# Shifted scores six ticks behind the maxima's scores in place of seven, and the maxima's rows sent from ScalarE's queue

## The chip, the cores and the metric

The kernel runs on one core of one Trainium2 chip. The metric is the device time of one execution in microseconds; the runs of the kernel before have a median of 1069.59 us (1068.0 to 1072.75, three runs). One further execution was profiled. All row times below are from that one.

The core has five engines that work side by side, each with its own queue of instructions in a fixed order: TensorE (PE, matrix products; PEld is its loading of weights), VectorE (DVE), ScalarE (ACT), GpSimd (POOL) and SyncE (SP, which here only issues DMA transfers). They wait for each other by semaphores.

## The reference

Two transformer layers over x of 2 sequences x 1024 tokens x 128 features, in float32:

- layer 0, first part: retention with 8 heads (scores times a decay), group norm, a silu gate, a projection, then a layer norm over the sum with x;
- layer 0, second part: causal attention with 16 heads of 8 features (with latent keys and values and rotary positions), followed by a mixture of four experts, of which each token takes the best one; layer norm;
- layer 1, first part: full attention with 16 heads of 8 features, two entries masked; layer norm;
- layer 1, second part: a product with a weight rounded to -1, 0, 1; layer norm.

The change lies in the two attentions:

```
scores = einsum('bhqd,bhkd->bhqk', q, k) * scale
weights = softmax(scores, axis=-1)
out = einsum('bhqk,bhkd->bhqd', weights, v)
```

## The kernel before

**Stages.** Retention goes over chunks of 128 tokens until about 240 us into the span. From there to the end one long chain of attention runs (`chain_tick`, L568 on): all steps of layer 0's causal attention for sequence 0, then sequence 1, then those of layer 1. A step is (layer a, sequence b, half of the tokens k, group g of four heads, h: which 256 queries). There are 64 steps: 32 in each layer. A step is cut into items: in layer 1 four for each step, in layer 0 one to four. There are 208 items (`s_items`, `t_items`), and the two lists give each step the same places.

**Why scores are computed twice.** Softmax needs the maximum of each query's scores. The kernel first makes scores with queries on the partitions (`score`, tiles named sc), and VectorE takes their maxima (`maxima`, L425 for blocks on the diagonal, L430 for the others). When all of a step's items are in, `shifts` (L437) makes `lowered`, the negated maxima. `turn` (L444) transposes them on TensorE, `enter` (L446 to L452) copies the transposed rows out of PSUM on ScalarE (m_rows) and sends them by DMA into a spare row of qT for each head. With that row in the product, the second set of scores comes out already shifted by the maximum, and with keys on the partitions: `shifted`, tiles sct. ScalarE takes their exponentials (`exps`, L485, tiles es), and `product` multiplies them with the values (tile acc).

**Order of a tick.** The order on all engines is the order in which the code issues. Tick t takes the scores of item t and the shifted scores of item t - AHEAD. It makes them in two halves, so that two heads of the one run beside two other heads of the other on TensorE: sc of heads 0, 1 with sct of heads 2, 3, then sct of heads 0, 1 with sc of heads 2, 3 (`together`). Each half is followed by its maxima on VectorE and its exponentials on ScalarE. Then comes `shifts`, if the step's last item was this one. At the end of the tick stands `product` for item t - AHEAD - 1. If a step's scores ended with tick t - 1, that product also holds its `turn`, into a free part of the same PSUM tile, and then its `enter`: after the matmuls of acc ScalarE first copies m_rows, then acc (to oT for a step's first pair, L518, else to part, L521, which GpSimd adds, L522). Last, `finish` of a step stands at t_last + AHEAD + 3: it transposes the sums (o_ps), and for all but the last block (layer 1, sequence 1, second half of the tokens) every second step does so, with four transposes and a copy on ScalarE (ot, L538). In the last block each step does, with two transposes and no such copy.

So a step whose last item is l enters at the end of tick l + 1. In a step of four items (first item f = l - 3), its rows are needed at the start of tick f + AHEAD.

**PSUM.** All these tiles, and those of the side work, come in turn from a ring of eight banks (`ring_of`). A tile waits until the eighth tile before it has been read.

**Side work.** Projections, the experts and the outputs are generators, stepped by `side_work` before each tick. Each has a first tick and a tick by which it is due; `ends` (which holds AHEAD) and `starts` give these in ticks. Their transfers (`spread` L280, expert weights L1219 and others) are issued on SP, whose queue is in the order of the code. Before the change the 64 DMAs of L452 stand in that queue too. The transfers issued by SP and ScalarE take eight semaphores in turn, over both queues, in the order of the code; an issue may have to wait for the transfer that used its semaphore before.

Of the kernel before, what the change touches and what calls it, by code (L numbers as in the profile page):

```python
# [20 lines left out]
BQ = QT * P  # L21
RH, RD, RV = 8, 64, 128
NG, GH, HD = 4, 4, 8
HW = 32
ONE, NEG0, NEG1 = 8, 9, 10
# [5 lines left out]
NH = NG * GH  # L31
VW = HD + 1
VN = (NH - 1) * VW + HW
AHEAD = 7


def _columns(*parts):
# [27 lines left out]
def block_kernel(  # L65
# [13 lines left out]
    nc = tc.nc  # L79
# [20 lines left out]
    for e in range(NE):  # L100
# [6 lines left out]
        out=ahead, in_=ahead, pattern=[[1, P]], compare_op=ALU.is_gt, fill=0.0,  # L107
# [68 lines left out]
    qT, kT = ([early.tile([P, NG, T], F32, name=f"{name}_0")] for name in ("qT", "kT"))  # L176
# [179 lines left out]
    def queries(i):  # L356

        a, b, k, g, h = steps[i]
        return k * (BT // BQ) + h
# [5 lines left out]
    for i, (a, b, k, g, h) in enumerate(steps):  # L365
# [4 lines left out]
        else:  # L370
# [5 lines left out]
            if sum(piece[2] for piece in rest_of) <= BT:  # L376
                at, pieces = 0, []
# [68 lines left out]
    def enter(i, tp):  # L446

        a, b, k, g, h = steps[i]
        rows_of = small.tile([GH * QT, P], F32, tag="m_rows", name="m_rows", bufs=2)
        nc.scalar.copy(rows_of, tp[: GH * QT])  # L450
        at = queries(i) * BQ
        nc.sync.dma_start(out=qT[b][ONE::HW, g, at : at + BQ], in_=rows_of)  # L452

    def diagonal_pair(n_item):
        i, pair = t_items[n_item]
# [42 lines left out]
    def product(n_item, entering):  # L498

        i, pair = t_items[n_item]  # L500
        a, b, k, g, h = steps[i]
        acc = slot("acc")
        if entering is not None:
            turn(entering, acc[:, BQ : BQ + P])
        for r, (lo, at_) in enumerate(pair_of(n_item)):
            for j in range(GH):
                at = (g * GH + j) * VW
                mm(
                    acc[hrows(j), lo:BQ], v_aug[b][:, 2 * pair + r, at : at + HW],
                    es[n_item][:, j, at_ : at_ + BQ - lo], start=r == 0, stop=r == 1,  # L510
                )
        if entering is not None:
            enter(entering, acc[:, BQ : BQ + P])
        if pair == 0 and (h == 0 or by_half(a, b, k)):
            sums[a, b, k, g] = pools["work"].tile([P, BT], F32, tag="oT", name="oT")
        sum_ = sums[a, b, k, g][:, h * BQ : (h + 1) * BQ]
        if pair == 0:
            nc.scalar.copy(sum_, acc[:, :BQ])  # L518
        else:
            part = pools["work"].tile([P, BQ], F32, tag="part", name="part", bufs=2)  # L520
            nc.scalar.copy(part, acc[:, :BQ])  # L521
            nc.gpsimd.tensor_tensor(sum_, sum_, part, ALU.add)  # L522
# [35 lines left out]
    def step_of(*step):  # L558
        return steps.index(step)

    def ends(a, b, k, h=NQ - 1):

        return t_last[step_of(a, b, k, NG - 1, h)] + AHEAD + 4

# [3 lines left out]
    def chain_tick(tick):  # L568
        si = tick if tick < n_items else None
        ti = tick - AHEAD if 0 <= tick - AHEAD < n_items else None  # L570

# [18 lines left out]
        if 0 <= si < n_items and s_last[s_items[si][0]] == si:  # L590
            entering = s_items[si][0]
        ai = tick - AHEAD - 1
        if 0 <= ai < n_items:
            product(ai, entering)
        elif entering is not None:
            tp = slot("m_ps")[:, :P]
            turn(entering, tp)
            enter(entering, tp)
        ai = tick - AHEAD - 3
        if 0 <= ai < n_items and t_last[t_items[ai][0]] == ai:  # L600
# [3 lines left out]
    with ExitStack() as rc:  # L604
# [29 lines left out]
        at, n = R_CONST["cs"]  # L634
# [802 lines left out]
    for b in range(B):  # L1437
# [13 lines left out]
        for k in range(NB):  # L1451
            light.append(
                Job(ends(0, b, NB - 1), starts(1, b, 0) + 1, attn_inputs(b, k), made[k : k + 1])
            )
    last_tick = n_items + AHEAD + 4
    for b in range(B):
# [164 lines left out]
```

## Time and profile before

| what | value |
|---|---|
| median of the runs | 1069.59 us (1068.0 to 1072.75) |
| profiled execution, its whole time | 1073.1 us |
| its span from first to last instruction | 1071.4 us |
| mean granted TensorE clock | 0.983 |
| SP's issue of m_rows (L452), 64 of them | 520 / 548 / 633 ns (least, median, most) |
| ACT copy of m_rows (L450), 59 of them out of acc | 237 / 254 / 256 ns |
| exps (L485), 832 | mean 587 ns |
| copy of acc to part (L521), 144 | mean 394 ns |
| maxima (L430), 640 | mean 682 ns |

How to read it: the page gives each engine's busy time, then the chain of work that ended last, traced back from the last instruction to what released each step. Groups are named by engine, line and "out<-in" with the program's tile names. A line in the timeline has the start from the span's beginning, the time it lasted, engine, line, operation, tiles, shapes and how many; in square brackets the idle time of the engine just before it and who ended it. Nearly all matmuls carry L86, which is a helper; the tile's name tells them apart. A float32 product appears as two matmuls. Lines with ACTq or SPq are issues in that engine's queue and are not counted as busy.

### The profile page before, as it was taken

The page shows a single profiled execution, that of the slowest core. Times are in us where ns is not written, and L with a number is a line of the kernel's source. Part 1 is how long each engine was busy: PE and PEld are TensorE (multiplying, and loading weights), DVE is VectorE, ACT ScalarE, POOL GpSimd, SP SyncE. Part 2 cuts the span into 40 slices and gives each one's busy share as a digit, 9 for nine tenths or more (in the row PEclk, how much of TensorE's full clock was granted, in tenths as well). Part 3 has the DMA queues.
Part 4 walks back from the last instruction along what each step waited for, and adds up shares of the span by engine and source line. Part 5 has one row for each costly group of instructions (what it writes and reads, how often), then busy time and mean ns, then how long its engine had stood idle before and what let it go on. Part 6 is the DMA issues. An engine that isn't in the chain of part 4 may idle for free.

```text
span 1071.4 us, 28823 instructions
## 1 busy us (share of the span) xinstructions
PE 1013.0 (95%) x11510; PEld 722.8 (67%) x11510; DVE 772.6 (72%) x1765; ACT 689.7 (64%) x1492; POOL 459.9 (43%) x626
## 2 busy tenths in 40 slices
PE   6999999997899999989999999999999999999995
PEld 5888888874565657756766667666766666666662
DVE  4666786667785877777676776777677888888861
ACT  3555544544576767667666776667677777777774
POOL 3466454533355665374544434454333222222222
PEclk9999999997899999999999999999999999999998
DMA  6522122110101032004211032003211000000000
GB/s 207 148 56 50 40 50 51 25 27 2 29 1 22 12 98 81 22 12 107 81 29 21 2 108 60 27 18 115 61 29 22 2 13 2 13 2 2 12 3 10
DMA packets 32214, 44.82 MB, mean 42 GB/s; under 512 B 4624, under 2 KB 18384, under 8 KB 31952
## 3 DMA queue, kind: packets, MB, share of 16 engines
q1 hardware_dynamic: 30816, 40.59, 14.3%
q0 software_dynamic: 1024, 2.10, 0.7%
q8 instruction: 91, 1.49, 0.6%
q14 instruction: 43, 0.35, 0.1%
q10 hardware_dynamic: 240, 0.29, 0.1%
HBM read 25.60 MB, written 4.39 MB: 28 GB/s over the span
## 4 chain that ended last, share of the span: by engine, by line
PE 71%; DVE 12%; POOL 6%; DMA 4%; ACT 3%; issue 2%; SPq 1%; POOLq 0%; DVEq 0%; ACTq 0%
PE sc L86 17%; PE acc L86 16%; PE sct L86 14%; DVE spare L425 3%; PE ph L86 3%; PE pmoe L86 2%; DVE parts L430 2%; PE pr L86 2%; PE pout L841 2%; PE py L86 2%; PE pv L86 1%; PE o_ps L211 1%; ACT es L485 1%; PE mpr L86 1%; PE acc L444 1%
## 5 line engine op out<-in xcount | busy, mean ns | idle before, releaser
L485 ACT ACTIVATE es<-sct 128x512 f32<-128x512 f32 (+1 forms) x832 | 418.8, 587 | 168.1 <-PE sct L86 150.0
L430 DVE TENSOR_REDUCE parts<-sc 128x1 f32<-128x512 f32 x640 | 397.3, 682 | 99.0 <-PE sct L86 86.4
L86 PE MATMUL sc<-kT,qT 32*128 32x512 f32 (+3 forms) x1792 | 421.6, 580 | 7.9 <-DVE parts L425 4.3
L86 PE MATMUL sct<-qT,kT 32*128 32x256 f32 (+1 forms) x3328 | 405.8, 385 | 3.8 <-DMA qT<-m_rows 3.7
L86 PEld LDWEIGHTS sct<-qT,kT 32*128 32x128 f32 x3328 | 288.2, 185 | 24.7 <-issue 6.3
L522 POOL TENSOR_TENSOR oT<-oT,part 128x256 f32<-128x256 f32 x144 | 104.6, 726 | 336.0 <-ACT part L521 334.9
L86 PE MATMUL acc<-es,v_aug 128*32 128x256 f32 (+1 forms) x3328 | 217.9, 378 | 12.2 <-DVE parts L430 6.1
L86 PEld LDWEIGHTS sc<-kT,qT 32*128 32x128 f32 x1792 | 153.9, 187 | 77.7 <-issue 20.8
L86 PEld LDWEIGHTS acc<-es,v_aug 128*32 128x32 f32 x3328 | 88.8, 109 | 106.2 <-DVE parts L430 40.4
L425 DVE CUSTOM_DVE_ANT_0 spare<-sc,causal 128x128 f32<-128x128 f32 (+3 forms) x256 | 125.7, 491 | 46.2 <-PE sct L86 13.0
L909 ACT ACTIVATE og<-pt,cols_sb 128x128 f32<-128x128 f32 x124 | 45.0, 467 | 43.3 <-PE pt L896 43.3
L493 POOL TENSOR_SCALAR_AFFINE_SELECT es<-es 128x512 f32<-128x512 f32 x64 | 40.3, 635 | 61.3 <-ACT es L485 59.5
L521 ACT COPY part<-acc 128x256 f32<-128x256 f32 x144 | 56.7, 394 | 10.8 <-PE acc L86 8.5
L140 POOL TENSOR_TENSOR rstd<-rstd,nhalf 128x4 f32<-128x4 f32 (+2 forms) x46 | 55.6, 1209 | 3.7
L778 POOL TENSOR_TENSOR qd<-qk,r_rest 128x512 f32<-128x512 f32 x16 | 20.3, 1271 | 48.5 <-DVE qk L775 45.6
L795 ACT COPY v<-pv 128x1024 f32<-128x1024 f32 x16 | 16.2, 1012 | 38.1 <-PE pv L86 38.1
L772 POOL TENSOR_TENSOR swap<-swap,r_cs 128x1024 f32<-128x1024 f32 x15 | 35.4, 2357 | 10.0 <-DMA swap<-plain 10.0
L86 PE MATMUL py<-r_wo,og 128*128 128x128 f32 x256 | 33.3, 286 | 2.2 <-DVE og L994 2.2
L86 PEld LDWEIGHTS py<-r_wo,og 128*128 128x128 f32 x256 | 31.5, 200 | 3.2 <-PE xn_ps L211 1.0
L841 PE MATMUL pout<-v,sm 128*128 128x128 f32 x256 | 31.5, 276 | 1.1 <-DVE sm L809 1.1
L86 PE MATMUL pg<-xT,r_wg 128*128 128x128 f32 x256 | 31.4, 276 | 1.1 <-ACT v L795 1.1
L86 PEld LDWEIGHTS ph<-xgT,e_w 128*128 128x128 f32 x224 | 27.1, 191 | 7.8 <-issue 4.9
(235 smaller groups left out, 1284.7 us busy)
## 6 DMA issues: line engine op xcount, KB each, us to landing
e_w<-in_m_w SPq DMA_DIRECT2D x56, 256.0 KB
swap<-plain SPq DMA_DIRECT2D x62, 128.0 KB
qT<-dense SPq DMA_DIRECT2D x32, 64.0 KB
kT<-dense SPq DMA_DIRECT2D x32, 64.0 KB
e_in<-by_expert SPq DMA_DIRECT2D x4, 448.0 KB
from_expert<-e_out SPq DMA_DIRECT2D x4, 448.0 KB
x<-in_x SPq DMA_DIRECT2D x4, 256.0 KB
mcs<-in_m_const SPq DMA_DIRECT2D x4, 256.0 KB
```

Source lines behind the costliest of these rows:

```text
L86: nc.tensor.matmul(o, lhsT, rhs, start=start, stop=stop)
L140: nc.gpsimd.tensor_tensor(r, r, nhalf[:, :n], ALU.pow)
L425: nc.vector.tensor_tensor_reduce(out=spare[:, :n], in0=sc[:, at : at + n], in1=causal[:, BT - n :], scale=1.0, scalar=-3.0e38, op0=ALU.add ...
L430: nc.vector.tensor_reduce(part, sc[:, at : at + n], AX.X, ALU.max)
L485: nc.scalar.activation(es[n_item][:, j, :n], sct[:, :n], AF.Exp, scale=scale)
L493: nc.gpsimd.affine_select(out=d, in_=d, pattern=[[0, GH], [1, P]], compare_op=ALU.is_ge, fill=0.0, base=0, channel_multiplier=-1,)
L521: nc.scalar.copy(part, acc[:, :BQ])
L522: nc.gpsimd.tensor_tensor(sum_, sum_, part, ALU.add)
L772: engine.tensor_tensor(swap[n], swap[n], table(n, 1), ALU.mult)
L778: nc.gpsimd.tensor_tensor(qd[n], rq[n], gq, ALU.mult)
L841: nc.tensor.matmul(pout[n][:, a, g, :], sm[:, a, g, :], v[n][:, 2 * g + a, :], start=opens(n) and g == 0, stop=True, skip_group_check=True,)
L909: nc.scalar.activation(to, of, AF.Identity, bias=bias_, scale=weight)
```

## The change

AHEAD goes from 7 to 6, so each tick's shifted scores, exponentials, products and finishes are those of an item one place later; `last_tick` and `ends`, which hold AHEAD, move by one tick. And the DMA that sends the rows of maxima is issued by ScalarE, right behind its own copy of m_rows and ahead of its copy of acc.

```diff
-AHEAD = 7
+AHEAD = 6
...
         rows_of = small.tile([GH * QT, P], F32, tag="m_rows", name="m_rows", bufs=2)
         nc.scalar.copy(rows_of, tp[: GH * QT])
         at = queries(i) * BQ
-        nc.sync.dma_start(out=qT[b][ONE::HW, g, at : at + BQ], in_=rows_of)
+        nc.scalar.dma_start(out=qT[b][ONE::HW, g, at : at + BQ], in_=rows_of)
```

In the built program, the tick in which a step of four items enters now holds the product of the second pair of the step before it (copied to part), where it held the first pair (copied to oT), and every second such tick also holds the finish of a step. Of the 64 issues on ScalarE, 36 carry a wait for an earlier transfer besides the wait for m_rows.

## The prediction

> **What bounds the kernel now.** I read the page first: who is busy, and what the chain that ended last is made of.
>
> ```profile
> PE 1013.0 (95%) x11510; PEld 722.8 (67%) x11510; DVE 772.6 (72%) x1765; ACT 689.7 (64%) x1492; POOL 459.9 (43%) x626
> PE 71%; DVE 12%; POOL 6%; DMA 4%; ACT 3%; issue 2%; SPq 1%; POOLq 0%; DVEq 0%; ACTq 0%
> ```
>
> TensorE (PE) carries 71% of the chain, ScalarE (ACT) 3%. The sums of busy time by stretch sharpen this for the second layer's attention: of the 180 us from 850 to 1030, PE is busy 179.21 and ACT 136.17. There a stall of PE is time lost, nearly one to one. The chain of waits over one tick in which a step's maxima enter:
>
> ```profile
> 946.18 0.22 PE acc L444
> 946.40 1.00 PE acc L86 x16
> 947.40 0.42 PE sc L86
> ```
>
> The timeline of the same tick, all engines:
>
> ```profile
> 947.47 0.25 ACT L450 COPY m_rows<-acc 8x128 f32<-8x128 f32 x1
> 947.63 0.36 ACT L518 COPY oT<-acc 128x256 f32<-128x256 f32 x1
> 947.75 0.53 SPq L452 DMA_DIRECT2D qT<-m_rows  x1
> ...
> 948.31 0.59 PE L86 MATMUL sc<-kT,qT 32*128 32x512 f32 x2
> ...
> 948.67 2.07 ACT L485 ACTIVATE es<-sct 128x512 f32<-128x512 f32 x4 [0.68 <-PE sct L86]
> ```
>
> A tick takes nine PSUM tiles from a ring of eight banks: sc 0,1, sct 2,3, then sct 0,1, sc 2,3, then acc. So the acc of one tick gives its bank to the eighth tile of the next tick, an sc of its second half. That half starts at 948.31 and the copy that frees the bank ends at 947.63+0.36 = 947.99. The slack is 0.32 us; ACT's own idle time before the next exps is 0.68.
>
> **What the change removes.** First, waits for the rows. The list of waits, and SP's part of the timeline before the longest of them:
>
> ```profile
> PE sct L86 <- DMA qT<-m_rows: 3.7, 3, 1.9
> ```
>
> ```profile
> 323.44 2.12 SPq L280 DMA_DIRECT2D qT<-dense  x3
> 325.66 0.56 SPq L452 DMA_DIRECT2D qT<-m_rows  x1
> ```
>
> That step's rows were copied by 320.5, but their issue stood behind spreads on SP until 325.66, so they landed about 3.5 us later and PE waited 1.85. On ACT's queue the issue no longer stands behind spreads or expert weights: -3.7 us. SP itself is freed of 64 waits for ACT; no row shows PE waiting for expert weights, so I give that nothing.
>
> Second, one tick. With six in place of seven, the first shifted scores join the scores of tick 6 and one tick at the end goes. The chain of waits there:
>
> ```profile
> 1044.42 1.09 PE sct L86 x16
> 1045.51 1.16 PE acc L86 x16
> ```
>
> That is 1.09+1.16 = 2.2 us of PE alone. The same matmuls move into the start, where PE sat idle 2.08 us before the transpose at 269.04 while VectorE did maxima, and so are hidden there. If that cover failed, they would run in pairs with score matmuls and still save about 0.9 (a paired tick 2.94, less its acc 1.01, against 1.09 for sct alone and some 1.7 for sc alone, my estimate from its 8 passes). So -2.2, between -3 and -0.9.
>
> **What it adds.** 64 DMA issues on ACT. SP's issues of m_rows last 548 ns in the median. The nearest rows for ACT's own queue are the two swap issues at the start:
>
> ```profile
> 9.47 1.01 ACT L751 COPY plain<-pr 128x1024 f32<-128x1024 f32 x1 [6.92 <-PE pr L86]
> 10.52 1.24 ACTq L758 DMA_DIRECT2D swap<-plain  x2
> 11.80 1.01 ACT L751 COPY plain<-pr 128x1024 f32<-128x1024 f32 x1 [1.31 <-PE pr L86]
> ```
>
> 0.59 and 0.60 us each; no ACT work runs during them, though that copy's wait is also put down to PE. The issue must wait until m_rows is written, which SP did 0.03 us after the copy's end. Behind the waiting issue stand the copy of acc, sometimes the copy of o_ps, and the next exps; who waits is PE. In the tick shown: m_rows ends at 947.72, the issue runs 947.75 to 948.30, the acc copy starts at 948.34 in place of 947.63, a delay of 0.71.
>
> A rule speaks for the change here. The Trainium skill ("DMA: Bandwidth & Descriptors", "Issuing engines are not separate DMA queues") says that spreading issues over engines saves only the sequencer's initiating time, usually small beside the transfer, and its "Anatomy of one DMA" gives a sequencer dispatch of about 50 ns, on GpSimd's path. With 50 ns the delay would be 0.09 (the copy's overlap lost) +0.03+0.05 = 0.17, inside the slack of 0.32: no stall. With the row it is 0.71. I take the row, because it is this form of instruction on ACT; 0.17 and 0.71 remain the two ends.
>
> Now the stall per step. With six ticks, the entering tick no longer carries pair 0 but pair 1, so the copy is the part of 0.41: 948.34+0.41 = 948.75, and PE starts 0.05 later (the shortest distance from an ACT end to a PE start that waited for it). 948.80-948.31 = 0.49. In every second entering tick the finish of the step two before now falls too: PE does four transposes (0.59) first, ACT adds the copy of o_ps (0.58), and that copy holds an sc bank. Counted from 947.33 as zero: m_rows 0.14, issue over at 0.97, part 1.01 to 1.38, o_ps copy to 1.96, the second half at 0.59+0.98 = 1.57. Stall 1.96+0.05-1.57 = 0.44. The mean is about 0.46.
>
> How many steps are exposed I took from the trace by following, behind each of the 64 m_rows copies, the ACT instruction whose end frees a bank. Second layer, 32 steps: 7 are covered, because expert or projection work of PE follows or no scores are left. 18 of the ordinary steps are exposed: 18 x 0.46 = 8.3. In the last block, finished half by half, 7 steps have two transposes (0.37) in front and no copy of o_ps: 1.42+0.05-1.35 = 0.12 each, 0.8. First layer: 14 of 32 exposed, 14 x 0.46 = 6.4; but VectorE stands in the chain there too, so I count two thirds, 4.3. Sum +13.4.
>
> **Small terms.** A tick less of lead for the rows: in the second layer the time from issue to first use is about 6 us, becomes about 3, and the landing takes 1.6 (the semaphore's last update). It stays hidden in ordinary ticks; where weights are moving, landings took 3.1 to 5 us, and a tick there 3.5 to 5: +0.5. ACT's issue also waits, in 36 of 64 places by the built order, for an earlier DMA on the same semaphore. All but a few were issued over 6 us before, and expert weights landed in about 2.5 to 3.5; the nearest was issued 4.1 before: +0.5.
>
> Sum: -3.7-2.2+13.4+1.0 = +8.5. From the profiled span, 1071.4+8.5 = 1079.9; with the 1.7 that lies around it (1073.1), 1081.6. That execution stands 3.5 above the median of the runs, so the median goes from 1069.59 to 1078.
>
> **Rivals.** Hidden issue: ACT's engine is not held for the length of the issue. Its place is the gap between m_rows and the acc copy; below about 0.3 us no bank is late. Then only the gains remain, -5.9+0.5: 1064. This ends on the faster side, and decides at that gap. For it: the skill's rule, and ACT's 3% of the chain. Against it: the ACT rows, and the slack of only 0.32. Chance 0.22, half of it faster by over 0.5%.
>
> Everything exposed: in the jobs' ticks too, with their order moved by a tick, ACT is late for PE: 64 x 0.46 = 29, and lanes or landings 1 to 2. 29+2-5.9: 1095, or half of that excess, 1087, where the jobs hide some. Chance 0.2.
>
> No effect (a stall that VectorE's lag takes up everywhere in the first layer and half of it in the second): 9.1/2+1-5.9 = -0.3, 1069. Chance 0.1; it speaks against it that PE is at 179.21 of 180.
>
> **How the numbers follow.** The forecast (stalls of 0.3 to 0.6 a step) has 0.48: 1073 to 1085. 0.5%, 5.3 us, is about what a measurement here can tell from no change. Faster (below 1064.2): 0.12. Same: the other half of the hidden issue 0.1, no effect 0.1, the low edge of the forecast 0.04, so 0.24. Slower: 0.64. The range, leaving out the fastest of the hidden cases and the slowest of the exposed: 1063 to 1089.
>
> **What would show it.** Right: in the timeline of an entering tick, 0.6 us or more between m_rows and part on ACT; in the list of waits PE behind ACT part or ot, some 13 us where there was next to none; PE behind qT<-m_rows near nothing; a drain shorter by a tick. Wrong: part follows m_rows within 0.3; or PE's new waits name the rows' DMA, which would make the lost tick of lead the cause.

## The result, and the profile after

The changed kernel takes 1083.7 us (median of five runs, 1082.33 to 1086.28) where the kernel before takes 1069.98 beside it: 1.0119 of the time, 95% interval 1.0091 to 1.0147. It is slower, by some 13.7 us or 1.2%; the forecast was 1078, in a range of 1063 to 1089. The profiled execution took 1083.66 us (span 1081.9), at the median of its runs; that of before stood 3 us above its own, so the two spans differ by 10.5 only.

The page of the changed kernel, the same two lines as before:

```profile
PE 1023.2 (95%) x11510; PEld 728.0 (67%) x11510; DVE 774.3 (72%) x1765; ACT 697.2 (64%) x1492; POOL 459.8 (42%) x626
PE 66%; DVE 15%; POOL 7%; DMA 4%; ACT 4%; issue 3%; SPq 1%; ACTq 0%; POOLq 0%; DVEq 0%
```

Nothing there tells what happened: PE is as busy as ever, and ACT's queue has 0% of the chain. The timeline of a tick in which a step's rows enter does (all engines; the tick's first sc started at 957.57):

```profile
957.70 0.26 ACT L450 COPY m_rows<-acc 8x128 f32<-8x128 f32 x1
957.99 0.54 ACTq L452 DMA_DIRECT2D qT<-m_rows  x1
...
958.56 0.37 ACT L521 COPY part<-acc 128x256 f32<-128x256 f32 x1 [0.61 <-ACT m_rows L450]
...
958.99 0.18 PEld L86 LDWEIGHTS sc<-kT,qT 32*128 32x128 f32 x1 [0.25 <-ACT part L521]
959.00 0.70 PE L86 MATMUL sct<-qT,kT 32*128 32x256 f32 x4
```

ACT stands idle for 0.61 us around its issue, the copy of acc starts 0.86 us after that of m_rows (0.16 before the change), and TensorE's load of weights for the next sc waits for that copy's end. The next tick starts at 961.06: 3.49 us after this one, where the tick shown of before took 2.93. The chain of waits over the same tick:

```profile
958.49 0.22 PE sct L86 x3
958.71 0.76 PE sc L86 x2
959.47 0.22 PE sct L86 x3
```

A piece of sc that takes about 0.2 in other ticks takes 0.76: the stall is recorded as a long matmul, not as a gap. The sums by stretch show how far this hides it. Columns: stretch, its length, then busy time and number of instructions of PE, PEld, DVE, ACT and POOL, the granted clock, and two of DMA. First the kernel before, then the changed one:

```profile
850.00:1030.00 180.00, 179.21 (x2308) 117.58 (x2308) 152.67 (x298) 136.17 (x301) 48.94 (x68) 1.00 0.02 7
```

```profile
850.00:1030.00 180.00, 179.08 (x2237) 116.45 (x2233) 147.06 (x285) 134.89 (x290) 49.75 (x68) 1.00 0.02 7
```

The busy time of PE is the same, but it holds 71 matmuls fewer. The Trainium skill ("Perfetto Trace Analysis", "Identifying the Most-Contended Engine") warns that matmul busy time is a bad measure of how near TensorE is to its peak, and points to the share of its weight loads (among others); here those fall by 1%, from 117.58 to 116.45, and the count of matmuls, lower by 3%, says it more clearly than either.

The list of waits, changed kernel (total us, times, longest):

```profile
ACT part L521 <- ACT m_rows L450: 23.1, 38, 0.6
...
ACT oT L518 <- ACT m_rows L450: 11.5, 19, 0.6
...
PEld sc L86 <- ACT part L521: 6.4, 28, 0.4
...
PE sct L86 <- DMA qT<-m_rows: 1.4, 3, 0.7
```

and the third of these in the kernel before:

```profile
PEld sc L86 <- ACT part L521: 2.8, 9, 0.8
```

The first two are new: 57 gaps of 0.6 on ACT. The waits for the rows fell from 3.7 to 1.4 us. The chain at the end of the changed kernel:

```profile
1052.36 1.61 DMA qT<-m_rows
...
1054.11 1.38 PE sct L86 x14
...
1056.49 1.09 PE sct L86 x16
1057.58 1.05 PE acc L86 x16
```

One such pair (1.09+1.05) has gone from the end, but the last step's rows now land on the chain: PE waited 0.34 us for them.

Set beside each other by the start of a tick's first matmul, the changed kernel is 4.9 us behind at tick 144 (of 208), 12.2 at tick 208, 10.5 at the end. So most of the loss, 7.3 us, comes with the last 64 ticks, which have the least side work.

### The profile page after: what moved, and what is told of

It is laid out like the page before. It is cut to its first block, busy times and chain, and to the rows that moved or that the text cites. A ratio compares the mean times of both kernels' runs of the same rounds, so it can differ in the third digit from the quotient of the medians.

```text
span 1081.9 us, 28716 instructions
## 1 busy us (share of the span) xinstructions
PE 1023.2 (95%) x11510; PEld 728.0 (67%) x11510; DVE 774.3 (72%) x1765; ACT 697.2 (64%) x1492; POOL 459.8 (42%) x626
## 4 chain that ended last, share of the span: by engine, by line
PE 66%; DVE 15%; POOL 7%; DMA 4%; ACT 4%; issue 3%; SPq 1%; ACTq 0%; POOLq 0%; DVEq 0%
PE sc L86 16%; PE acc L86 15%; PE sct L86 12%; DVE spare L425 4%; DVE parts L430 3%; PE ph L86 3%; PE pmoe L86 2%; PE pr L86 2%; PE pout L841 2%; ACT es L485 2%; PE pv L86 1%; PE py L86 1%; PE o_ps L211 1%; PE psc L86 1%; PE acc L444 1%
## 5 line engine op out<-in xcount | busy, mean ns | idle before, releaser
L86 PE MATMUL sc<-kT,qT 32*128 32x512 f32 (+3 forms) x1792 | 433.1, 575 | 10.6 <-DVE parts L425 5.1
L86 PE MATMUL sct<-qT,kT 32*128 32x256 f32 (+1 forms) x3328 | 413.0, 386 | 1.4 <-DMA qT<-m_rows 1.4
L86 PEld LDWEIGHTS sct<-qT,kT 32*128 32x128 f32 x3328 | 284.5, 185 | 20.2 <-ACT part L521 1.5
L86 PEld LDWEIGHTS sc<-kT,qT 32*128 32x128 f32 x1792 | 159.8, 185 | 90.7 <-DVE parts L430 18.7
L518 ACT COPY oT<-acc 128x256 f32<-128x256 f32 x64 | 24.9, 390 | 14.6 <-ACT m_rows L450 11.5
```

The costliest lines, as they stand in the source:

```text
L86: nc.tensor.matmul(o, lhsT, rhs, start=start, stop=stop)
```

## The experiments

Theory 1: the issue holds ScalarE ahead of its copy of acc, and TensorE waits for that bank. Theory 2: the lost tick costs, by less lead for the rows or by the finish that falls into the entering tick. Theory 3: the cost lies in the transfer (ScalarE's ring, the shared semaphores, the landing). All ratios are against the kernel before on the same chip; absolute times differ from chip to chip.

**The queue alone** (act7).

```diff
-AHEAD = 6
+AHEAD = 7
```

> The new queue alone: rows issued by ScalarE, still seven ticks. Theory 1 (the issue holds ScalarE for 0.54 us ahead of the copy of acc, and TensorE waits for the bank): TensorE's stall is the same as in the changed kernel, some 15 us gross, less the 3.7 us of waits for the rows that go: 1080 to 1083 us. Theory 2 (the lost tick costs, by less lead or by the finish falling into the entering tick): nearly nothing is left but the gain of 3.7 us: 1066 us.

1.0141 (1.0118 to 1.0165). No wait for rows is left, and TensorE waits for ScalarE's copies:

```profile
PEld sc L86 <- ACT oT L518: 9.0, 26, 2.1
```

An entering tick lasts 3.50 us where it lasted 2.94. The queue costs the whole of it without the lost tick; against theory 2. It came out a little above what I expected, and in the profile one tick (93) is 3.9 us longer than before: at 627.78 the rows were written, but their issue started only at 629.49, because it waited for the semaphore of an earlier transfer of expert weights. The copy of acc behind it was held for that too:

```profile
ACT oT L518 <- DMA e_w<-in_m_w: 2.3, 1, 2.3
```

That is a piece of theory 3. The changed kernel has no such wait: each of its 64 issues started 0.03 us after its rows were written.

**The lost tick alone** (sp6).

```diff
-AHEAD = 7
+AHEAD = 6
```

> Six ticks alone: rows still issued by SyncE. Theory 1: no ScalarE gap, a tick less at the end (-2 us), but the four steps whose rows were held up behind spreads and weights on SyncE now lack one more tick of 3.3 to 4 us each: TensorE behind the rows' DMA grows from 3.7 to about 17 us, 1076 to 1084 us. Theory 2: besides that every step pays for the order, above 1085 us, with the entering ticks of the last 180 us longer than 3.1 us.

1.0112 (1.0089 to 1.0134). The list of waits:

```profile
PE sct L86 <- DMA qT<-m_rows: 13.4, 4, 5.3
```

SP's part of the timeline in front of one of the four waits:

```profile
390.96 2.82 SPq L280 DMA_DIRECT2D kT<-dense  x4
393.89 0.56 SPq L452 DMA_DIRECT2D qT<-m_rows  x1
```

Rows that stand behind four spreads on SyncE miss a tick of lead. The three ticks with the long waits last 18.1 us longer together than in the same order of work with the rows on ScalarE's queue (act6_last below), which is more than the 15.1 us that lie between the two forms at tick 208. So this half of theory 2, less lead for the rows, holds while the rows are on SyncE. The entering ticks of the last part keep their length (2.94 at tick 149). So each half of the change alone is slower by more than 1%, for different reasons: six ticks need another queue for the rows, and that queue, at that place, costs as much.

**The issue behind the copy of acc** (act6_late, and with seven ticks act7_late).

```diff
-        nc.scalar.dma_start(out=qT[b][ONE::HW, g, at : at + BQ], in_=rows_of)
+        return lambda: nc.scalar.dma_start(
+            out=qT[b][ONE::HW, g, at : at + BQ], in_=rows_of
+        )
...
-            enter(entering, acc[:, BQ : BQ + P])
+            send = enter(entering, acc[:, BQ : BQ + P])
...
             nc.scalar.copy(part, acc[:, :BQ])
             nc.gpsimd.tensor_tensor(sum_, sum_, part, ALU.add)
+        if entering is not None:
+            send()
...
```

> The change, but with ScalarE's issue moved behind its copy of acc. The same instructions, so the same ScalarE time. Theory 1: the bank comes free 0.7 us earlier and the issue falls into ScalarE's idle time of 0.6 us before the next exps: the stall goes, 1064 to 1067 us. Theory 2, and also a theory in which ScalarE's total load counts: no change against the changed kernel, 1080 to 1084 us.

> As the last, with seven ticks. Theory 1: only the waits for the rows (3.7 us) are gone against the kernel before: 1066 us, about 2 us above the six-tick form. Theory 2: 1066 us too, but then the six-tick form with the late issue stands at 1080.

Six ticks 1.0000 (0.9983 to 1.0018), seven ticks 0.9974 (0.9959 to 0.9988). Moving one instruction of ScalarE past its neighbour takes the stall away, though ScalarE's load is the same. The timeline of an entering tick, six ticks:

```profile
952.43 0.26 ACT L450 COPY m_rows<-acc 8x128 f32<-8x128 f32 x1
952.60 0.36 ACT L523 COPY part<-acc 128x256 f32<-128x256 f32 x1
...
952.72 0.54 ACTq L452 DMA_DIRECT2D qT<-m_rows  x1
```

The issue begins 0.03 us after m_rows is written, while part is still being copied. But the six-tick form stayed behind the forecast of 1064 to 1067 us: it should have been 0.2% to 0.5% faster than before. In the last part every second entering tick was still long, 3.34 us at tick 153 against 2.98 in the six-tick form with rows on SyncE.

**The issue at the end of the tick** (act6_last): the same, with `send()` called behind `finish`.

```diff
...
         if 0 <= ai < n_items and t_last[t_items[ai][0]] == ai:
             finish(t_items[ai][0])
+        if send is not None:
+            send()
```

> Six ticks, the issue on ScalarE at the end of the tick, behind the copy of the sums that a finish makes too. With the issue right behind the copy of acc every second entering tick of the last part stayed 0.22 to 0.36 us too long. Theory 1: that was the copy of the sums (ot) standing behind the issue, and it goes: about 2.6 us below that form, 0.997 to 0.998 of before. If the six-tick order itself were the cost: 1.000 again.

0.9973 (0.9952 to 0.9994), and tick 153 lasts 2.98. What was left came from the copy of the sums (ot), which stood behind the issue. This and the seven-tick form are the fastest kernels here, both faster than the kernel before, by about 0.27%. Between them no difference can be told; so whether six ticks are worth the 2 us at the end is not settled by the times. In the profile, from tick 208 to the end, the six-tick form gains 2.4 us on before; it keeps four waits for rows, 2.5 us.

**A pause without a transfer** (sp7_pause600, sp7_pause200, sp7_pause64): the kernel before, with a copy of n columns into a tile that nobody reads.

```diff
             enter(entering, acc[:, BQ : BQ + P])
+            pause = small.tile([P, 600], F32, tag="pause", name="pause", bufs=1)
+            nc.scalar.copy(pause, mcs[:, :600])
```

> The kernel before (seven ticks, rows on SyncE), with a copy of 128x600 into an unused tile on ScalarE between its copy of the rows and its copy of acc: a pause of about 0.7 us there with no transfer on ScalarE's queue at all. Theory 1 (the held ScalarE is the whole cost): as with the issue there, 0.56 us of stall in each exposed tick, 1.4% to 1.8% slower than before, a little above the form with the queue alone, because the 3.7 us of waits for the rows stay. Theory 3 (the cost lies in the transfer: ScalarE's ring, shared semaphores, landing): no change, within 0.3%.

1.0110 (1.0089 to 1.0131), less than expected: the pause came out shorter than the issue, and the one long wait of the form with the queue alone is not in it. No transfer is on ScalarE's queue, and most of the loss is there: theory 3 falls as the main cause. The timeline on ScalarE:

```profile
941.57 0.25 ACT L450 COPY m_rows<-acc 8x128 f32<-8x128 f32 x1
941.73 0.69 ACT L515 COPY pause<-mcs 128x600 f32<-128x600 f32 x1
942.32 0.36 ACT L520 COPY oT<-acc 128x256 f32<-128x256 f32 x1
```

The copy of acc starts 0.75 us after that of m_rows, 0.59 later than before.

> The same with a copy of 128x64, a pause of about 0.2 us, which is inside the slack of 0.32 us. Theory 1: no stall, within 0.3% of before. If ScalarE's total load or the number of its instructions counted, a proportional part: 0.2 of 0.7, so 0.4% to 0.5% slower.

1.0001 (0.9984 to 1.0019), entering ticks of 2.94 (tick 149). ScalarE's load alone does not count. The profile of this run also shows how far two profiles of like kernels differ: its span is 2.5 us below that of before, though the entering ticks are equal; 2.2 us of that have come about by tick 144.

> The kernel before with a pause of 128x200 on ScalarE, about 0.26 us between its copy of the rows and its copy of acc. It tells apart two readings of the slack. If the bank is needed when the sc matmul starts (0.32 us, the forecast's reading): no stall, entering ticks of 2.93 to 2.94 us. If it is needed 0.18 us earlier, when that matmul's weights are loaded (slack 0.14): entering ticks of 3.05 to 3.07 us, and 0.1% to 0.5% slower than before in all.

The timeline on ScalarE:

```profile
951.10 0.26 ACT L450 COPY m_rows<-acc 8x128 f32<-8x128 f32 x1
951.26 0.35 ACT L515 COPY pause<-mcs 128x200 f32<-128x200 f32 x1
951.52 0.36 ACT L520 COPY oT<-acc 128x256 f32<-128x256 f32 x1
```

0.26 us later than before, and the tick lasts 3.04: 0.10 of stall where the forecast's reading of the slack gave none. (The whole time, 1.0011, 0.9991 to 1.0031, doesn't resolve it.)

**Two issues** (act7_twice): the queue alone, with the same rows sent a second time to an unused tile.

```diff
         nc.scalar.dma_start(out=qT[b][ONE::HW, g, at : at + BQ], in_=rows_of)
+        again = small.tile([GH * QT, P], F32, tag="again", name="again", bufs=2)
+        nc.scalar.dma_start(out=again, in_=rows_of)
```

> Seven ticks, the issue on ScalarE ahead of the copy of acc, and a second one right behind it that sends the same rows to an unused tile. Theory 1: the gap grows from 0.70 to about 1.28 us, all of the second issue is past the slack, and steps that were covered become exposed: 64 x 0.58 = 37 us more at most, 25 to 37 us above the form with one issue, so 1.037 to 1.05 of before. Theory 3: the second transfer is 4 KB more on an idle ring: within 0.5% of the form with one issue.

1.0473 (1.0450 to 1.0496), as theory 1 has it, 33 points in a thousand above one issue. The timeline on ScalarE at tick 149:

```profile
872.22 0.25 ACT L450 COPY m_rows<-acc 8x128 f32<-8x128 f32 x1
872.51 0.59 ACTq L452 DMA_DIRECT2D qT<-m_rows  x1
873.14 0.65 ACTq L454 DMA_DIRECT2D again<-m_rows  x1
873.83 0.37 ACT L520 COPY oT<-acc 128x256 f32<-128x256 f32 x1 [1.35 <-DMA qT<-m_rows]
```

The gap is 1.35 us, more than the 1.28 that I had put down. The bracket names a transfer, but the rows show the gap filled by the two issues, each starting within 0.05 us of what stands before it.

The same tick of the same step (tick 149: second layer, second sequence) in these kernels gives the law:

| delay of ScalarE's copy of acc against before, us | kernel | tick, us | longer by |
|---|---|---|---|
| 0 | before | 2.94 | |
| 0.15 | pause of 64 columns | 2.94 | 0 |
| 0.26 | pause of 200 | 3.04 | 0.10 |
| 0.59 | pause of 600 | 3.37 | 0.43 |
| 0.70 | one issue (seven ticks; six ticks) | 3.50; 3.50 | 0.56 |
| 1.45 | two issues | 4.24 | 1.30 |

Beyond a slack, TensorE's stall is the delay less 0.14 to 0.16 us, whatever made the delay. Counted by the end of the copy, which behind an issue took 0.01 us longer, the slack is 0.16 in each of the four rows with a stall.

## Why the prediction was right, and where its sizes were off

**The waits for rows, -3.7.** Right in kind: the two worst on SyncE are gone. Of 3.7 us 1.4 are left: the third step of before waits as it did (0.67, before 0.59), and two more come in, one in the second layer (0.36) and the last step (0.34). The rows of the first two took 4.7 and 4.4 us from issue to landing, beside spreads and expert weights on SyncE; those of the last took 1.6. The small term of +0.5 for less lead was a third of the 1.4. The other small term, +0.5 for issues that wait for an earlier transfer, came to nothing here; with seven ticks one such wait was costly.

**The tick at the end, -2.2.** From tick 208 to the last product of the attention the changed kernel takes 2.5 us less than before, with the 0.34 for the last rows inside; so this term was right. From there to the end it takes 0.7 us more, which makes -1.7 for the whole; the form with the issue last in its tick has -2.4. Why the stretch behind the attention was longer in this profile I did not follow.

**ScalarE is held for the issue.** This was the choice between 0.17 and 0.71, and the row was right: 0.70. The two places of the Trainium skill that the forecast weighed against the row do not fit this issue. It is not small beside its transfer: 0.54 us of the 1.6 from issue to landing. And the dispatch of about 50 ns, given for another path, is not what it costs: 528 to 1110 ns, 536 in the median.

**The stall per step, 0.46.** Measured 0.56 (tick 149; forecast 0.49), 0.58 with a finish in the same tick (153: 3.56 against 2.98; forecast 0.44), 0.29 to 0.30 in the last block (ticks 189, 197, 205; forecast 0.12). The term that was mis-sized is the slack. I took 0.32 us, from the copy's end to the start of the sc matmul, and took off the 0.05 that TensorE needs to start again: 0.27 in effect. The runs show 0.16. (In the 0.49 the copy stands with 0.41, in the 0.44 with 0.37; it took 0.37, so the first had a small error the other way.) The trace puts the wait on PEld, the load of that matmul's weights. In the tick shown of before, that load starts ahead of the matmul at 948.31:

```profile
948.10 0.19 PEld L86 LDWEIGHTS sc<-kT,qT 32*128 32x128 f32 x2
```

That is 0.11 after the end of the copy at 947.99, and a load that had to wait starts 0.05 after it (958.99 against 958.56+0.37 = 958.93 in the changed kernel). So the slack to the load's start would be about 0.06, to the matmul's 0.27, and 0.16 lies between. That the load is what waits is shown by the rows; why the slack has this size is not.

**How many steps are exposed.** Against the form with the issue last in the tick, which has the same order of work on TensorE, the change loses 7.5 us in the last 64 ticks, where I had 4.5 (8 x 0.46 + 7 x 0.12), and 5.8 in the first 144, where I had 8.9. In the last part eight entering ticks (145 to 173) are longer by 0.55 to 0.58, three (177 to 185) by 0.45 to 0.56, and four of the last block by 0.29 to 0.30; one (201) is not. In the first part 23 ticks are longer by 0.26 to 0.72, 11.3 us together. Against that, others are shorter by up to 0.9 (54, 94, 61, 118 among them), 4.3 us together, and 1.6 us come from before tick 8, where the changed kernel was ahead. Why those ticks are shorter I did not follow.

**The sum.** By the profiles +10.5 for +8.5, by the medians +13.7 for +8.5. Stalls of 13.4 were forecast; 13.9 is what the two six-tick profiles differ by (by the ratios, 1.0119 and 0.9973, it is 15.6). That these come so close is luck: the forecast had the last 64 ticks 3.0 us too low and the first 144 ticks 3.1 too high, the second of which is hardly more than two profiles of like kernels differ by. The other terms were forecast at -4.9; in the form with the issue last in its tick they came to -3.5 by the profiles. The medians show 3 us more than the profiles because the profiled execution of before was that much slower than its own median.

**The rivals.** The hidden issue falls: the gap it was to be judged by is 0.61 us on ACT's record, not below 0.3, and the point where it decides lies at a delay of about 0.16. No effect falls: nothing in the last part took the stall up. Everything exposed needed 29 us of stalls; the profiles show 13.9.

## What to carry to other kernels

A DMA issue on ScalarE's queue took 0.54 us in its place in the order here, even for 4 KB, and the copy behind it was late by 0.70. So put an issue behind whatever another engine is waiting for (here one line further down, which turned 1.4% slower into 0.26% faster with seven ticks, and 1.2% slower into no difference with six; at the end of the tick, 0.27% faster), and judge by the slack of that one copy, not by the engine's busy share of 64%. Where a buffer is handed back to TensorE, do not count the slack to the start of the matmul alone, since its weight load waits too, and look for the stall in the distance between ticks, because a stalled matmul is shown as a busy one.

## What the runs showed of the hardware that was not expected

ScalarE's sequencer issues a DMA while its own earlier copy is still running (952.72, inside the copy from 952.60 to 952.96), so the issue cost nothing where nothing behind it was ready: the next exps came at 953.57 after 0.62 us of idle time, against 0.68 in the tick shown of before, and tick 149 kept its 2.94 us. And TensorE's busy time read 179.35 of 180 us in the fastest six-tick form (2324 matmuls), 179.08 in the changed kernel (2237), and still 178.15 with two issues in each entering tick (2117).
